# Layer 0 of a convolution-and-attention program: DVE's use of PE's products one block of taps later, spread factors copied by ACT, splits and Newton's step on DVE

## The chip, the cores and the metric

The kernel runs on one core of one Trainium2 chip. The metric is the device time of one execution in microseconds (us). One program computes both layers; nothing but inputs and the output passes the host. The engines are named as in the profile: PE (TensorE's matmuls; PEld is its weight loads), DVE (VectorE), ACT (ScalarE), POOL (GpSimd), SP (SyncE, which issues most DMAs).

## The reference

The input is eight images of 256 channels and 32 x 32 pixels, in fp32. The program computes layer 0 and then layer 1 (a causal attention over 1024 tokens and a dense feed-forward block of eight experts). The change concerns layer 0 alone:

```python
def _ln(x, w, b):                      # norm over channels, no mean subtracted
    r = lax.rsqrt(jnp.mean(x * x, axis=1, keepdims=True) + LN_EPS)
    return x * r * w[:, None, None] + b[:, None, None]

def _attention(x, ...):
    qkv = _bn(_conv1x1(x, qkv_w), ...).reshape(B, NH, 2 * KD + HD, N)   # NH 4, KD 32, HD 64, N 1024
    q, k, v = ...
    attn = softmax(einsum('bhkn,bhkm->bhnm', q, k) * SCALE)
    out = einsum('bhdm,bhnm->bhdn', v, attn).reshape(B, Cc, H, W)
    out = out + _bn(_dwconv3(v_img, pe_w), ...)        # depthwise 3x3 of v
    return _bn(_conv1x1(out, proj_w), ...)

def _edffn(x, pi_w, dw_w, fft_p, po_w):
    x = _dwconv3(_conv1x1(x, pi_w), dw_w)              # 256 -> 1024 channels, depthwise 3x3
    x = gelu(x[:, :512]) * x[:, 512:]
    x = _conv1x1(x, po_w)                              # 512 -> 256
    # every 8x8 patch: rfft2, times fft_p, irfft2
    ...

x = x + gamma1 * _attention(_ln(x, norm1_w, norm1_b), ...)
x = x + gamma2 * _edffn(_ln(x, norm2_w, norm2_b), ...)
```

## The kernel before

**Order.** Every engine call of layer 0 goes through a wrapper (`InOrder`: pe, dve, act, pool) that keeps the instructions of each engine in the order in which Python issues them; the wrapper's line, L71, is therefore the line of all of them in the profile, and groups are told apart by the names of their tiles. The order is made by generators. Each `yield` ends a step. `main_of(i)` is the main stream of image i, nearly all of it PE's work: norm2 of image i-1 (`norm2`), the spectrum of image i-2 (`spectrum`), attention of image i (`attend`) woven with the queries and keys of image i+1 (`queries_keys`), then `values(i+1)` woven with `finish(i)`, then the projection (`project`). The side stream is the depthwise convolutions on DVE: `v_conv(i)` of v, and `hidden(i-1, ...)` of the 1024 hidden channels. A tap is one `scalar_tensor_tensor` over 128 x 1024; eight of them make one channel group, and between them `open_group` issues the group's 1x1 convolution (ph) on PE, which ACT evacuates twice (into hpad and into x or conv). `level(main, side, share)` runs one step of the main stream, then draws taps from the side until the cost booked for DVE reaches `share` times that booked for PE.

**What DVE does for PE.** Between taps DVE also uses what PE has just produced. The operation is issued in the same main step as PE's matmuls, and so ahead of that step's taps:

- `rms_norm` (norm1 in `queries_keys`, norm2): the means of squares (ms) are brought to partitions by a transpose (`factors`: tpy), POOL computes the root by pow and one Newton step and splits it in two parts (r: a rounded one and the rest), PE transposes it back (`turned`: tr), spreads it over the partitions (`apply`: rbn), and DVE multiplies image, weight and spread factor (xn). `gaps` is the number of extra yields between `factors` and `turned`.
- attention: `products()` issues, one pair of key blocks behind the exponentials (pT), the products po and the sums. `close` of a chunk of 256 queries copies them (pu, ss) and returns three later steps: `turn` (PE transposes the sums, tps; DVE's reciprocal sr; ACT's accumulate, which also writes sr; POOL's split rs), `back` (PE transposes rs, trs; ACT copies it, rsT), `spread` (PE spreads the factors, rb; DVE multiplies pu and adds it to o). The four chunks' steps run within `attend`, the last chunk's in `finish`.
- `queries_keys`: each product pq is taken by ACT (hi) and DVE (lo, the rest that hi loses by rounding).
- `spectrum`: pz (PE), zf (ACT), pf (PE), gf (DVE: times the filter), py (PE), t (DVE: the residual).

**PSUM.** The pool `ps_m` has two slots of one bank, under one tag ("mm"); ph, pq, ms, tpy, tr, rbn, tps, trs, rb, tpv, pf, py and half of pp share them. A slot is free again when the last instruction that was issued for its tile is done. The scores, pz and the rest of pp lie in `ps_s`, po and the sums in `ps_o`.

Image 0 has no hidden channels beside it; `queries_keys(0)` and `values(0)` run before the loop, and a tail (norm2 of the last image, the last two spectra, and the first matrix products of layer 1) behind it.

Of the kernel before, what the change touches and what calls it, by code (L numbers as in the profile page):

```python
# [103 lines left out]
def conv_attn_hybrid_kernel(  # L104
# [340 lines left out]
    def together(main, side, ratio):  # L445
# [10 lines left out]
        for _ in side or ():  # L456
            pass

    def level(main, side, share):

        p0, d0 = pe.spent, dve.spent
        for _ in main:
            while side is not None and dve.spent - d0 < share * (pe.spent - p0):
                step = next(side, False)
                if step is None:
                    break
                if step is False:
                    side = None
        for _ in side or ():
            pass  # L470

# [4 lines left out]
    with ExitStack() as l0:  # L476
# [141 lines left out]
        def rms_norm(b, wname, xn, gaps=0):  # L618

            of = {}  # L620

            def squares(h):
                of[h] = []
                for k in range(KC):
                    sq = one.tile([P, HALF], F32, tag="full", name="sq", bufs=2)
                    act.activation(sq, t[b][:, k, h * HALF : (h + 1) * HALF], AF.Square)
                    of[h].append(sq)

            def means(h):
# [12 lines left out]

            def factors():
                yr = of.pop("yr")
                tp = ps_m.tile([P, 2, P], F32, tag="mm", name="tpy")
                for h in range(2):
                    pe.transpose(tp[:, h, :], yr[:, h, :], ident)
                y = small.tile([P, 2, nq], F32, tag="y", name="y")
                act.copy(y, tp[:, :, ::KD])

                r = of["r"] = small.tile([P, 2, 2, nq], F32, tag="r", name="r")
                a = small.tile([P, 2, nq], F32, tag="a", name="a")
                pool.tensor_tensor(a, y, mhalf.rearrange("p (a b) -> p a b", a=2), ALU.pow)
                pool.tensor_mul(y, y, a)
                pool.tensor_mul(y, y, a)
                pool.tensor_scalar(y, y, -0.5, 1.5, ALU.mult, ALU.add)
                pool.tensor_mul(a, a, y)
                pool.tensor_copy(r[:, :, 0, :].bitcast(F32R), a)
                pool.tensor_sub(r[:, :, 1, :].bitcast(F32R), a, r[:, :, 0, :])

            def turned():
                r = of.pop("r")
                tr = ps_m.tile([2 * nq, 2, P], F32, tag="mm", name="tr")
                for h in range(2):
                    pe.transpose(tr[:, h, :], r[:, h].rearrange("p a b -> p (a b)"), ident)
                of["rT"] = small.tile([2 * nq, 2, P], F32R, tag="rT", name="rT", bufs=1)
                act.copy(of["rT"], tr)

            def apply(h):
                rb = ps_m.tile([P, HALF], F32, tag="mm", name="rbn")  # L670
                for i in range(nq):
                    pe.matmul(
                        rb[:, i * P : (i + 1) * P], pick_n[:, i : i + 1].to_broadcast([2 * nq, P]), of["rT"][:, h, :],
                        start=True, stop=True,
                    )
                hs = slice(h * HALF, (h + 1) * HALF)
                for k in range(KC):
                    dve.scalar_tensor_tensor(xn[:, k, hs], t[b][:, k, hs], col(wname, k), rb, ALU.mult, ALU.mult)

            squares(0)  # L680
            yield 0.2
            means(0)
            squares(1)
            yield 1.0
            means(1)
            level()
            yield 1.0
            factors()
# [30 lines left out]
        def queries_keys(b):  # L719
# [3 lines left out]


            att[b] = {"xn": one.tile([P, KC, N], F32, tag="xn", name="xn")}
            yield from rms_norm(b, "n1w", att[b]["xn"], 1)
            for g in range(2):
                hi = one.tile([P, N], F32R, tag="hi", name="hi")
                lo = one.tile([P, N], F32, tag="lo", name="lo")
# [1 line left out]

                def take(hs, pq):
                    act.activation(hi[:, hs], pq, AF.Identity, bias=bias)
                    dve.scalar_tensor_tensor(lo[:, hs], pq, bias, hi[:, hs].bitcast(F32), ALU.add, ALU.subtract)

                yield from qkv_group(b, g, take)
                parts = att[b][g] = [dram.tile([P, N], F32, tag=f"part{g}{r}", name="part", bufs=2) for r in range(2)]
# [54 lines left out]
        def attend(b):  # L792
# [25 lines left out]
            def close(c, po, sm):  # L818
# [8 lines left out]
                def turn():  # L827
                    tp = ps_m.tile([P, nt, P], F32, tag="mm", name="tps")
                    for i in range(nt):
                        pe.transpose(tp[:, i, :], ss[:, i * P : (i + 1) * P], ident)  # L830
                    r = small.tile([P, nt, NH], F32, tag="sr", name="sr", bufs=2)
                    dve.reciprocal(r, tp[:, :, ::KD])
                    flat = r.rearrange("p a b -> p (a b)")
                    act.activation(flat, flat, AF.Copy, accum_out=accs[:, 1, b, c : c + 1])
                    rs = of["rs"] = small.tile([P, nt, 2, NH], F32, tag="rsp", name="rs", bufs=2)
                    pool.tensor_copy(rs[:, :, 0, :].bitcast(F32R), r)
                    pool.tensor_sub(rs[:, :, 1, :].bitcast(F32R), r, rs[:, :, 0, :])

                def back():
                    tr = ps_m.tile([2 * NH, QC], F32, tag="mm", name="trs")  # L840
# [21 lines left out]
            late = []  # L862

            def products():
                for one_ in late:
                    product(*one_[:4])
                    if one_[2] == nj - 1:
                        todo.extend(close(one_[4], *one_[:2]))
                late.clear()

            for c in range(N // QC):
                qs = slice(c * QC, (c + 1) * QC)
# [2 lines left out]
                for j0 in range(0, nj, 2):  # L875
                    new = []
                    for j in (j0, j0 + 1):
                        ks = slice(j * P, (j + 1) * P)
                        s = ps_s.tile([P, NH, QC], F32, tag="s", name="s")
                        for hd in range(NH):  # L880
                            pe.matmul(s[:, hd, :], kst[:, hd, ks], qst[:, hd, qs], start=True, stop=True)
                        pT = two.tile([P, NH, QC], F32, tag="pT", name="pT", bufs=4)
                        act.activation(pT, s, AF.Exp)
                        new.append((po, sm, j, pT, c))
                    products()
                    late.extend(new)
                    later()
                    yield 3.5
            products()
            att[b]["rest"] = todo  # L890
            yield 2.6
# [172 lines left out]
        def spectrum(b):  # L1064
# [19 lines left out]
            def second(z):  # L1084
                pf = ps_m.tile([P, 2, C], F32, tag="mm", name="pf")
                pe.matmul(pf, dft, z, start=True, stop=True)
                gf = two.tile([P, 2, C], F32, tag="ev", name="gf", bufs=3)
                dve.tensor_mul(gf, pf, filt.unsqueeze(1).to_broadcast([P, 2, C]))
                return gf

            def third(n, gf):
                py = ps_m.tile([P, KC, PS, 2, W // 2], F32, tag="mm", name="py")
                for g in range(KC):
                    for k in range(2):
                        pe.matmul(py[:, g, :, k, :], gf[:, k, g * P : (g + 1) * P], idft, start=True, stop=True)
                for g in range(KC):
                    tb = t[b][:, g, n * BAND : (n + 1) * BAND]
                    dve.scalar_tensor_tensor(
                        tb, py[:, g].rearrange("p r k c -> p (r k c)"), col("gam2", g), tb, ALU.mult, ALU.add
                    )  # L1100

            z, gf = {}, {}
            for n in range(nb + 2):
# [91 lines left out]
        head = weave(norm2(B - 1), spectrum(B - 2), 1)  # L1195
        while not ready2.get(B - 1):
            next(head)

        def rest():
# [682 lines left out]
```

## Time and profile before

| | |
|---|---|
| median of three runs | 3304.81 us (3293.08 to 3309.06) |
| the profiled execution | 3302.11 us, its span 3300.4 us |
| mean granted TensorE clock | 0.966 |
| PE busy | 3043.3 us, 92% of the span, 17462 instructions |
| PEld busy | 2066.2 us, 63% |
| DVE busy | 2346.7 us, 71%, 3710 instructions |
| ACT busy | 1395.4 us, 42%, 2168 instructions |
| POOL busy | 361.1 us, 11%, 482 instructions |
| DMA | 130.60 MB, 40 GB/s on average |

Layer 0 takes the first 43% of the span, to about 1420 us. In its steady state an image takes 164.6 us, from one projection's last residual to the next (648.49 to 813.06 us).

Times in lines of the profile are in us; in a line of the timeline stand the start, the duration (of all instructions if there are several, xN), the engine, the line, the operation, the tile written and the tiles read, the shape, and in brackets the engine's idle time ahead of it with the instruction that ended it. In a line of groups stand, behind the bar, the busy time, the mean duration in ns, and the group's idle time ahead with its main releaser. The granted clock is 1.00 at full speed.

### The profile page before, as it was taken

To read this page: it belongs to the slowest core of one execution; us is meant where nothing else is said; L and a number is where in the kernel's file an instruction comes from. 1 tells how busy PE (TensorE), PEld (TensorE's weight loads), DVE (VectorE), ACT (ScalarE), POOL (GpSimd) and SP (SyncE) were. 2 spreads that over 40 slices of the span, in tenths; PEclk is the share of its full clock that TensorE was granted. 3 is DMA by queue.
4 is the path that set the end of the run, shared out by engine and by line. 5 is a ranking of instruction groups with operands and counts; after the bars stand their busy time and mean duration, and the time that the engine had idled before them with its cause. 6 is when DMAs were issued, how large, how long until landed. Compare 5 with 4: busy or idle time off the path is not lost.

```text
span 3300.4 us, 43194 instructions
## 1 busy us (share of the span) xinstructions
PE 3043.3 (92%) x17462; PEld 2066.2 (63%) x17462; DVE 2346.7 (71%) x3710; ACT 1395.4 (42%) x2168; POOL 361.1 (11%) x482
## 2 busy tenths in 40 slices
PE   5998999999998998769999998999999999999999
PEld 3554555454555455346565665678777777778787
DVE  1377877787877786835544444688888877888887
ACT  2554454545454544323333332344444444444443
POOL 1121212020212010001122212400000000000000
PEclk8998999999999999879999999899999999999999
DMA  4202030303030300030111101100000000000000
GB/s 146 71 8 77 26 77 27 77 27 77 27 77 27 77 14 7 16 136 26 47 44 39 39 26 52 42 24 20 20 20 20 32 16 23 20 20 26 13 7 13
DMA packets 44596, 130.60 MB, mean 40 GB/s; under 512 B 3862, under 2 KB 12134, under 8 KB 40550
## 3 DMA queue, kind: packets, MB, share of 16 engines
q1 hardware_dynamic: 44390, 127.78, 12.5%
q8 instruction: 139, 2.28, 0.3%
q14 instruction: 67, 0.55, 0.1%
HBM read 77.17 MB, written 50.59 MB: 39 GB/s over the span
## 4 chain that ended last, share of the span: by engine, by line
PE 49%; DVE 5%; ACT 1%; POOL 1%; issue 1%; DMA 0%; SPq 0%; ACTq 0%; POOLq 0%; DVEq 0%
PE pm L71 12%; PE pa L71 12%; PE q L71 11%; PE s L71 4%; PE po L71 3%; PE pk L71 2%; PE pv L71 2%; DVE nm L71 1%; DVE zt L71 1%; DVE pr L71 1%; DVE st L71 1%; ACT pr L71 1%; PE tp L71 1%; PE tpz L71 1%; PE tpt L71 1%
## 5 line engine op out<-in xcount | busy, mean ns | idle before, releaser
L71 ACT ACTIVATE h<-h,bn_o,bn_s 128x512 f32<-128x512 f32 x384 | 308.6, 813 | 631.2 <-DVE h L71 631.1
L71 DVE SCALAR_TENSOR_TENSOR x<-hpad,vec,x 128x1024 f32<-128x1024 f32 x248 | 317.1, 1283 | 39.9 <-ACT x L71 32.9
L71 DVE SCALAR_TENSOR_TENSOR conv<-hpad,vec,conv 128x1024 f32<-128x1024 f32 x256 | 329.3, 1293 | 15.4 <-ACT conv L71 8.9
L71 PE MATMUL pm<-h,w 128*128 128x512 f32 (+1 forms) x768 | 318.2, 523 | 0.0
L71 ACT ACTIVATE pT<-s 128x1024 f32<-128x1024 f32 x256 | 247.4, 1024 | 71.8 <-PE s L71 71.8
L71 PE MATMUL po<-pT,vT 128*32 128x256 f32 x4096 | 273.6, 385 | 0.0
L71 PE MATMUL ph<-xn,piw 128*128 128x512 f32 x512 | 244.7, 615 | 3.1 <-DVE xn L71 1.6
L71 PE MATMUL s<-kk,z 128*128 128x512 f32 x512 | 243.0, 602 | 0.6 <-DVE pr L71 0.6
L71 DVE SCALAR_TENSOR_TENSOR o<-vpad,pe_w,o 128x1024 f32<-128x1024 f32 x128 | 163.6, 1283 | 45.6 <-ACT o L71 42.4
L71 PEld LDWEIGHTS pm<-h,w 128*128 128x128 f32 x768 | 146.4, 191 | 75.4 <-issue 61.8
L71 PE MATMUL s<-qst,kst 128*128 128x256 f32 x1024 | 176.0, 314 | 14.6 <-DMA kst<-part 13.2
L71 DVE TENSOR_TENSOR h<-h,wb 128x1024 f32<-128x1024 f32 x128 | 156.8, 1225 | 43.2 <-ACT h L71 43.2
L71 DVE TENSOR_TENSOR h<-pa,first 128x512 f32<-128x512 f32 x128 | 88.3, 690 | 132.6 <-PE pa L71 129.1
L71 PEld LDWEIGHTS po<-pT,vT 128*32 128x32 f32 x4096 | 120.8, 110 | 85.8 <-issue 4.1
L71 DVE TENSOR_TENSOR h<-h,first 128x256 f32<-128x256 f32 x384 | 164.5, 428 | 13.2
L71 PEld LDWEIGHTS s<-qst,kst 128*128 128x128 f32 x1024 | 137.5, 193 | 47.9 <-issue 43.2
L71 ACT ACTIVATE hpad<-ph,pi_o 128x512 f32<-128x512 f32 x126 | 86.8, 689 | 184.6 <-PE ph L71 184.3
L71 PEld LDWEIGHTS ph<-xn,piw 128*128 128x128 f32 x512 | 92.7, 194 | 109.6 <-issue 94.4
L71 PE MATMUL pz<-pow__116,hid 128*128 128x256 f32 x512 | 134.7, 418 | 26.7 <-DVE hid L71 26.7
L71 PE MATMUL sums<-pT,ones 128*32 128x256 f32 x2048 | 158.2, 381 | 0.0
L71 PE MATMUL pa<-tz,ws 128*128 128x256 f32 x512 | 154.6, 384 | 0.0
L71 PE MATMUL pa<-ze,w 128*128 128x256 f32 x512 | 153.3, 382 | 0.0
(264 smaller groups left out, 5792.7 us busy)
## 6 DMA issues: line engine op xcount, KB each, us to landing
qst<-part SPq DMA_DIRECT2D x32, 512.0 KB, 8.7
kst<-part SPq DMA_DIRECT2D x32, 512.0 KB, 15.2
t<-in_x_dram SPq DMA_DIRECT2D x8, 1024.0 KB, 4.8
part<-hi SPq DMA_DIRECT2D x16, 512.0 KB, 2.7
part<-lo SPq DMA_DIRECT2D x16, 512.0 KB, 3.0
td<-t SPq DMA_DIRECT2D x8, 1024.0 KB, 4.9
t<-td SPq DMA_DIRECT2D x8, 1024.0 KB, 4.8
ze<-zd SPq DMA_DIRECT2D x16, 512.0 KB, 3.9
```

The lines of the kernel that those rows point to most:

```text
L71: return self._tc.keep_in_program_order(method(*args, **kwargs))
```

## The change

It touches layer 0 only, in four ways.

1. DVE's operations on PE's products are put on a list (`deferred`) instead of being issued at once. `level` empties the list (`flush`) after the taps of each step; where there are no taps, `flushed` empties it ahead of each next step. Deferred are: the Newton step and the split of norm2's root, xn, lo, the reciprocal of the softmax's sums with its split, the multiply and add of `spread`, gf, and t<-py.
2. ACT copies the spread factors to SBUF (rbs, from rbn and from rb), and DVE reads them there: 64 more ACT copies of 128 x 512.
3. The split of the reciprocal moves from POOL to DVE, ahead of ACT's accumulate. The Newton step and the split of norm2's root move from POOL to DVE; pow stays on POOL. norm1's root stays on POOL. In all DVE has 112 instructions more and POOL 112 fewer; PE's number is unchanged.
4. `gaps` becomes 2 instead of 1 for norm1 and 0 instead of 2 for norm2. `products()` issues one product behind each exponential instead of two behind two, and pT has three buffers instead of four.

```diff
+    deferred = []
+
+    def flush():
+        while deferred:
+            deferred.pop(0)()
+
+    def flushed(steps):
+        for us in steps:
+            flush()
+            yield us
+
     def level(main, side, share):
...
                 if step is False:
                     side = None
+            flush()
         for _ in side or ():
             pass
...
                 pool.tensor_tensor(a, y, mhalf.rearrange("p (a b) -> p a b", a=2), ALU.pow)
-                pool.tensor_mul(y, y, a)
-                pool.tensor_mul(y, y, a)
-                pool.tensor_scalar(y, y, -0.5, 1.5, ALU.mult, ALU.add)
-                pool.tensor_mul(a, a, y)
-                pool.tensor_copy(r[:, :, 0, :].bitcast(F32R), a)
-                pool.tensor_sub(r[:, :, 1, :].bitcast(F32R), a, r[:, :, 0, :])
+
+                def root(eng):
+                    eng.tensor_mul(y, y, a)
+                    eng.tensor_mul(y, y, a)
+                    eng.tensor_scalar(y, y, -0.5, 1.5, ALU.mult, ALU.add)
+                    eng.tensor_mul(a, a, y)
+                    eng.tensor_copy(r[:, :, 0, :].bitcast(F32R), a)
+                    eng.tensor_sub(r[:, :, 1, :].bitcast(F32R), a, r[:, :, 0, :])
+
+                if gaps:
+                    root(pool)
+                else:
+                    deferred.append(lambda: root(dve))
...
+                rbs = two.tile([P, HALF], F32, tag="rbn", name="rbs", bufs=1)
+                act.copy(rbs, rb)
                 hs = slice(h * HALF, (h + 1) * HALF)
-                for k in range(KC):
-                    dve.scalar_tensor_tensor(xn[:, k, hs], t[b][:, k, hs], col(wname, k), rb, ALU.mult, ALU.mult)
+
+                def scale():
+                    for k in range(KC):
+                        dve.scalar_tensor_tensor(xn[:, k, hs], t[b][:, k, hs], col(wname, k), rbs, ALU.mult, ALU.mult)
+
+                deferred.append(scale)
...
-            yield from rms_norm(b, "n1w", att[b]["xn"], 1)
+            yield from rms_norm(b, "n1w", att[b]["xn"], 2)
...
-                    dve.scalar_tensor_tensor(lo[:, hs], pq, bias, hi[:, hs].bitcast(F32), ALU.add, ALU.subtract)
+
+                    def low():
+                        dve.scalar_tensor_tensor(lo[:, hs], pq, bias, hi[:, hs].bitcast(F32), ALU.add, ALU.subtract)
+
+                    deferred.append(low)
...
-                    r = small.tile([P, nt, NH], F32, tag="sr", name="sr", bufs=2)
-                    dve.reciprocal(r, tp[:, :, ::KD])
-                    flat = r.rearrange("p a b -> p (a b)")
-                    act.activation(flat, flat, AF.Copy, accum_out=accs[:, 1, b, c : c + 1])
-                    rs = of["rs"] = small.tile([P, nt, 2, NH], F32, tag="rsp", name="rs", bufs=2)
-                    pool.tensor_copy(rs[:, :, 0, :].bitcast(F32R), r)
-                    pool.tensor_sub(rs[:, :, 1, :].bitcast(F32R), r, rs[:, :, 0, :])
+
+                    def invert():
+                        r = small.tile([P, nt, NH], F32, tag="sr", name="sr", bufs=2)
+                        dve.reciprocal(r, tp[:, :, ::KD])
+                        rs = of["rs"] = small.tile([P, nt, 2, NH], F32, tag="rsp", name="rs", bufs=2)
+                        dve.tensor_copy(rs[:, :, 0, :].bitcast(F32R), r)
+                        dve.tensor_sub(rs[:, :, 1, :].bitcast(F32R), r, rs[:, :, 0, :])
+                        flat = r.rearrange("p a b -> p (a b)")
+                        act.activation(flat, flat, AF.Copy, accum_out=accs[:, 1, b, c : c + 1])
+
+                    deferred.append(invert)
...
-                    o = att[b]["o"][:, :, qs]
-                    dve.tensor_mul(pu, pu, rb)
-                    dve.tensor_add(o, o, pu)
+                    rbs = two.tile([P, NH // 2, QC], F32, tag="rbs", name="rbs", bufs=1)
+                    act.copy(rbs, rb)
+
+                    def divide():
+                        o = att[b]["o"][:, :, qs]
+                        dve.tensor_mul(pu, pu, rbs)
+                        dve.tensor_add(o, o, pu)
+
+                    deferred.append(divide)
...
             def products():
-                for one_ in late:
+                if late:
+                    one_ = late.pop(0)
                     product(*one_[:4])
                     if one_[2] == nj - 1:
                         todo.extend(close(one_[4], *one_[:2]))
-                late.clear()
...
-                        pT = two.tile([P, NH, QC], F32, tag="pT", name="pT", bufs=4)
+                        new.append((po, sm, j, s, c))
+                    for i, (po, sm, j, s, _) in enumerate(new):
+                        pT = two.tile([P, NH, QC], F32, tag="pT", name="pT", bufs=3)
                         act.activation(pT, s, AF.Exp)
-                        new.append((po, sm, j, pT, c))
-                    products()
+                        new[i] = (po, sm, j, pT, c)
+                        products()
...
-            yield from rms_norm(b, "n2w", xn2[b], 2)
+            yield from rms_norm(b, "n2w", xn2[b])
...
-                dve.tensor_mul(gf, pf, filt.unsqueeze(1).to_broadcast([P, 2, C]))
+                deferred.append(lambda: dve.tensor_mul(gf, pf, filt.unsqueeze(1).to_broadcast([P, 2, C])))
...
+                def put():
+                    for g in range(KC):
...
+                deferred.append(put)
...
+            flush()
             nc.sync.dma_start(t_d[b], t[b])
...
-        for _ in queries_keys(0):
+        for _ in flushed(queries_keys(0)):
...
-        for _ in values(0):
+        for _ in flushed(values(0)):
...
             next(head)
+            flush()
...
-        together(rest(), hidden(B - 1, (), (2,), alone=True), 1.0)
-        for _ in spectrum(B - 1):
+        together(flushed(rest()), hidden(B - 1, (), (2,), alone=True), 1.0)
+        for _ in flushed(spectrum(B - 1)):
```

More of the change, by code (lines that the diff above doesn't have):

```diff
@@ L647, in factors @@
                     pe.transpose(tp[:, h, :], yr[:, h, :], ident)
-                y = small.tile([P, 2, nq], F32, tag="y", name="y")
+                y = small.tile([P, 2, nq], F32, tag="y", name="y", bufs=2)
                 act.copy(y, tp[:, :, ::KD])
-                r = of["r"] = small.tile([P, 2, 2, nq], F32, tag="r", name="r")
-                a = small.tile([P, 2, nq], F32, tag="a", name="a")
+                r = of["r"] = small.tile([P, 2, 2, nq], F32, tag="r", name="r", bufs=2)
+                a = small.tile([P, 2, nq], F32, tag="a", name="a", bufs=2)
                 pool.tensor_tensor(a, y, mhalf.rearrange("p (a b) -> p a b", a=2), ALU.pow)
-                pool.tensor_mul(y, y, a)
-                pool.tensor_mul(y, y, a)
-                pool.tensor_scalar(y, y, -0.5, 1.5, ALU.mult, ALU.add)
-                pool.tensor_mul(a, a, y)
-                pool.tensor_copy(r[:, :, 0, :].bitcast(F32R), a)
-                pool.tensor_sub(r[:, :, 1, :].bitcast(F32R), a, r[:, :, 0, :])
+                def root(eng):
[9 more added lines that the diff above has]
+                    deferred.append(lambda: root(dve))
             def turned():
@@ L888, in attend @@
                     yield 3.5
+            products()
             products()
@@ L1095, in third @@
                         pe.matmul(py[:, g, :, k, :], gf[:, k, g * P : (g + 1) * P], idft, start=True, stop=True)
[L1096 to L1100, printed above, removed]
+                def put():
+                    for g in range(KC):
+                        tb = t[b][:, g, n * BAND : (n + 1) * BAND]
+                        dve.scalar_tensor_tensor(
+                            tb, py[:, g].rearrange("p r k c -> p (r k c)"), col("gam2", g), tb, ALU.mult, ALU.add
+                        )
+                deferred.append(put)
             z, gf = {}, {}
@@ L1197, in conv_attn_hybrid_kernel @@
             next(head)
+            flush()
         def rest():
```

## The prediction

> **What bounds the kernel now.** I read the table of windows first, for one period of layer 0 in the steady state (image 4: 660 to 825 us; columns: window, its length, then busy us and count of PE, PEld, DVE, ACT and POOL, granted clock, DMA share, GB/s).
>
> ```profile
> 660.00:825.00 165.00, 149.72 (x1244) 88.20 (x1243) 129.79 (x130) 82.57 (x126) 26.13 (x26) 0.96 0.19 52
> ```
>
> PE works 149.7 of 165 us; DVE 129.8, ACT 82.6. The period is PE's work plus PE's waits, so filling DVE's idle 35 us is worth nothing by itself. Second, the groups by line over 170 to 1300 us, where the idle time ahead of PE stands with what ended it:
>
> ```profile
> L71 PE MATMUL trs<-ident,rs 128*8 128x128 f32 x56 | 12.6, 313 | 55.5 <-POOL rs L71 55.5
> L71 PE MATMUL tr<-ident,r 128*8 128x128 f32 x26 | 5.8, 310 | 19.5 <-DVE gf L71 19.5
> ```
>
> 75 of PE's idle us sit at two transposes, of the softmax's inverse sums (trs) and of the norm's root (tr). Third, the timeline. Stall C, in finish():
>
> ```profile
> 787.59 3.70 PE L71 MATMUL pq<-xn,qkvw 128*128 128x512 f32 x8
> 791.13 0.38 PE L71 MATMUL tps<-ident,ss 128*128 128x128 f32 x2
> 795.76 0.20 DVE L71 RECIPROCAL sr<-tps 128x8 f32<-128x8 f32 x1
> 796.35 0.85 POOL L71 CAST rs<-sr 128x8 fp32r<-128x8 f32 x1 [1.59 <-ACT sr L71]
> 797.29 1.25 POOL L71 TENSOR_TENSOR rs<-sr,rs 128x8 fp32r<-128x8 f32 x1
> 798.59 0.59 PE L71 MATMUL trs<-ident,rs 128*8 128x128 f32 x2 [5.87 <-POOL rs L71]
> 798.98 5.52 PE L71 MATMUL pq<-xn,qkvw 128*128 128x512 f32 x8
> ```
>
> The sums are transposed at 791.5; the reciprocal starts 4.2 later, behind queued taps, then POOL takes 2.1. Behind the stall the same eight matmuls take 5.52 instead of 3.70: half the clock, 1.8 us more. Stall B, chunk 0 of attention:
>
> ```profile
> 718.73 1.25 POOL L71 TENSOR_TENSOR r<-a,r 128x8 fp32r<-128x8 f32 x1
> 719.93 0.18 POOL L71 CAST rs<-sr 128x8 fp32r<-128x8 f32 x1
> 720.19 1.11 POOL L71 TENSOR_TENSOR rs<-sr,rs 128x8 fp32r<-128x8 f32 x1
> 721.36 0.59 PE L71 MATMUL trs<-ident,rs 128*8 128x128 f32 x2 [3.03 <-POOL rs L71]
> 721.74 4.89 PE L71 MATMUL ph<-xn,piw 128*128 128x512 f32 x8
> ```
>
> The split rs stands behind norm1's root on POOL. Stall A, in norm2:
>
> ```profile
> 667.37 1.13 POOL L71 TENSOR_TENSOR r<-a,r 128x8 fp32r<-128x8 f32 x1
> 668.35 0.69 DVE L71 TENSOR_TENSOR gf<-pf,filt 128x512 f32<-128x512 f32 x1
> 669.18 0.38 PE L71 MATMUL tr<-ident,r 128*8 128x128 f32 x2 [3.25 <-DVE gf L71]
> ```
>
> The releaser shown is gf, but tr reads r, which POOL finished at 668.5. A, B and C recur in images 2 to 6 within 0.03 us; A also in image 7.
>
> **Removed: B.** Copy and subtraction of the split move to DVE, ahead of ACT's accumulate. Reciprocal and two tiny operations come behind the taps of their step, about 6.4 us after tps, and trs is reached 7.5 after it. 5 x 3.03 = 15.1. Three of the five B's are followed by a slow ph group (4.89 against 3.70): 3 x 1.2 = 3.6. Together 18.7.
>
> **Removed: C.** Three taps (1.3 each) run, then the reciprocal (0.20) and two operations of 128x8; PE arrives about 0.6 us later, a thin margin. 5 x (5.87 + 1.8) = 38.4. In image 1 the like stall is 7.20 and I leave 2.2 of it: 5.0; a 1.58 gap at 248.71 there, where the slot of rb was held by a late DVE multiply, goes with ACT's copy, with the clock behind it 4.9 in all (1.58 + 3.3). Waits of 1.02 and 0.85 elsewhere: 2. Sum of gains: 18.7 + 38.4 + 9.9 + 2 = **69**.
>
> **Added: PSUM held longer.** tps lies in the pool ps_m of two slots. Its reader is now issued after the step's taps, and two of these taps' steps issue ph matmuls that need slots of that pool. With one slot taken, a ph or the next product must wait until ACT has emptied the ph issued just before. The order of instructions shows such a wait three times an image in images 1 to 7 (the second ph or tpy behind tps of chunks 0 to 2, or the rbn there): 21. The price is that loop, seen where it already runs at the tail of layer 0 (PE's end is 1317.56, tpw starts 1319.17):
>
> ```profile
> 1317.76 0.69 ACT L71 ACTIVATE hpad<-ph,pi_o 128x512 f32<-128x512 f32 x1 [0.36 <-PE ph L71]
> 1318.34 0.77 ACT L71 ACTIVATE x<-ph,dw_o,vec 128x512 f32<-128x512 f32 x1
> 1319.17 0.66 PE L71 MATMUL tpw<-ident,lin 128*128 128x128 f32 x4 [0.56 <-ACT x L71]
> ```
>
> 1.6 us x 21 = 33.6; between 0 (ACT done in time because PE is late) and 2.5 each (ACT busy with an exp of 1.02 first). Whether the clock drops too is the open term. Gaps of 1.58 and 2.15 cost 6.8 and 3.4 us of half clock in this trace, gaps of 1.34, 1.02 and 0.85 none, and one of 3.08 none:
>
> ```profile
> 246.46:249.87 3.41, 1.83 (x13) 0.97 (x6) 3.38 (x6) 0.00 (x0) 0.00 (x0) 1.00 0.00 0
> 249.87:253.29 3.42, 3.42 (x10) 1.92 (x9) 3.35 (x4) 1.36 (x2) 0.00 (x0) 0.50 0.00 0
> ```
>
> PE was busy 1.83 of the first 3.41 us and ran the next at 0.50. Whether a gap tips the clock thus goes by where it falls in such a window. I let one in three do so, at the 1.8 of stall C: 7 x 1.8 = 12.6 (ends: 0, and 21 x 3.3 = 69). Sum: **46**.
>
> The Trainium skill ("TensorE: Matmul & The Clock Gate", Part 1 and "HAM oscillation") lets PE fall to 4/8 after an idle window of about 3.4 us and asks for no gaps over that. By it the 1.6-us gaps would cost only themselves, and the sum would be 12.6 lower; the 0.50 behind the 1.58 gap above speaks against it. The same page's "A second HAM failure mode: psum-queue depth-cycling" speaks against this change: there short idles from cycling through PSUM banks were enough to make the clock oscillate.
>
> **Moved: norm2's root (A).** pow stays on POOL (2.25), six operations go to DVE, into the flush behind seven taps: 656.23 + 7 x 1.31 = 665.4, gf 0.69, six operations of 128x8 at about 0.2 (nearest rows: the 128x8 reciprocal 0.20; ten times that on POOL is the far end), so tr at 667.2, 2.0 earlier. But both dropped yields bring rbn and py close behind tr, where pz x8 lay. Now rbn waits for ACT's rT (about 0.5), py for the new copy of rbn (586 ns plus signal, 0.9) and the second rbn for gf (1.3): 2.7. Net +0.7 x 6 = 4.2. A does not go, it is cut in pieces.
>
> **Added: 64 ACT copies of 128x512.** 64 x 0.586 = 37 us on an engine idle for half the period: hidden, except where PE stands right behind: tpv waits for rbs in finish, 0.4 x 7 = 2.8; image 0's norm and values, without taps to fill in, +1.4; the last norm2 and spectrum, +2.9. DVE gains nothing by reading SBUF: its multiply takes 706 ns on o from SBUF and 686 on rb from PSUM. Two more 128x8 operations per close and six per norm2, under 3 us an image, fall into DVE's idle 35; without that cover 8 x 3 = 24. Products issued one by one behind each exp, with three pT instead of four, and low, gf and put a flush later move no wait of PE that I could find: 0, or +1 for each of seven images. The third yield now ahead of norm1's tr gives its root, which stays on POOL, one step more. POOL's queue only gets shorter; of the DMAs only each image's store td<-t stands a flush later, and nobody waits for it: 0.
>
> **Sum.** -69 + 46 + 4.2 + 2.8 + 4.3 = -11.5, against the profiled execution's 3302.1 (span 3300.4): **3290.6 us**, -0.35%. That execution lies 2.7 below the median 3304.8. A measurement of this kernel can tell about 0.5%, 16.5 us, from no change. Layer 1 has no edit: 0.
>
> **Rivals.** *Faster*: the PSUM waits find ACT ready or cost no clock (-12.6: 3278), and A closes as well (6 x (3.24 + 1.6) = 29 less: 3249). For it: 1.34, 1.02 and 0.85 left the clock alone. Against: DVE's chain and gf in A. *Slower, one mechanism*: every PSUM wait tips the clock. At 1.8 each 21 x 1.8 = 37.8 instead of 12.6: 3316; at 3.3, 3347. It decides from 14 of the 21 on (11.5 / 1.8 = 6.4 beyond 7). For it: B tipped 3 of 5 and A also runs pz at 5.30 against 3.62. Against: 1.6 fits inside half a window. *Slower by late DVE*: the reciprocal misses C's margin of 0.6 and C stays: -11.5 + 38.4, so 3329. *Nothing happens* is the case itself: gains and new waits cancel.
>
> **How the numbers follow.** Forecast case 0.45 (own range 3282 to 3300), the faster ones 0.33 (3278: 0.23, 3249: 0.10), every wait tipping the clock 0.14, C staying 0.08. Range: 3252 leaves out most of 3249; 3330 leaves out 3347 and the upper half of C's case. Faster by over 0.5%: most of 0.33 and a fifth of 0.45, 0.38. Slower: half of 0.14, 0.08 and a little for unseen waits, 0.18. Within: 0.44.
>
> **What would show it.** Right: trs without idle ahead of it in images 2 to 6 and pq at 3.70 behind it; PE gaps of about 1.6 before ph, tpy or rbn released by ACT, three an image; tr still with gaps around it; DVE's 128x8 operations near 0.2. Wrong: trs still released by DVE at 3 us or more; PSUM gaps absent, or with 0.50 behind most; a period far from 163 (now 164.6).

## The result, and the profile after

The changed kernel takes 3314.61 us, median of 20 runs, against 3309.05 of 20 runs of the kernel before: ratio 1.0023, 95% interval 1.0014 to 1.0033. The forecast was 3290.6, 11.5 us less than before; the time rose by 5.6. It lies inside the stated range and inside the 0.5% that the prediction called the least a measurement can tell, but the interval of 20 runs lies wholly above 1: the kernel became a little slower, not faster.

The page of the changed kernel shows the moved work and nothing of a gain: 112 instructions more on DVE, 112 fewer on POOL, 64 more on ACT, and PE busy for the same share. A window of 165 us over about the same stretch of image 4 as the one shown of before has PE at work for 149.56 us, where before it was 149.72.

```profile
span 3306.7 us, 43215 instructions
...
PE 3047.5 (92%) x17462; PEld 2071.9 (63%) x17462; DVE 2366.0 (72%) x3822; ACT 1435.5 (43%) x2232; POOL 275.9 (8%) x370
```

```profile
656.30:821.30 165.00, 149.56 (x1236) 88.15 (x1235) 130.66 (x142) 87.28 (x134) 14.00 (x13) 0.96 0.19 52
```

The groups over 170 to 1300 us of the changed kernel (busy, mean ns, idle time ahead with its releasers):

```profile
L71 PE MATMUL ph<-xn,piw 128*128 128x512 f32 x448 | 210.6, 601 | 14.6 <-ACT conv L71 11.6 <-ACT x L71 2.9
...
L71 PE MATMUL py<-idft,gf 128*128 128x128 f32 x192 | 32.7, 323 | 7.0 <-ACT rbs L71 4.1 <-DVE gf L71 2.8
...
L71 PE MATMUL rbn<-rT,pick_n 8*128 8x128 f32 x104 | 21.6, 337 | 7.7 <-ACT conv L71 7.2 <-ACT rT L71 0.5
L71 PE MATMUL ms<-sq,ones 128*32 128x128 f32 x448 | 18.9, 288 | 17.9 <-ACT x L71 17.9
...
L71 PE MATMUL trs<-ident,rs 128*8 128x128 f32 x56 | 10.7, 272 | 5.3 <-DVE rs L71 5.3
L71 PE MATMUL tpy<-ident,yr 128*128 128x128 f32 x26 | 5.6, 297 | 11.1 <-ACT x L71 7.2 <-ACT yr L71 3.8
L71 PE MATMUL tr<-ident,r 128*8 128x128 f32 x26 | 5.4, 290 | 23.1 <-DVE r L71 21.6 <-ACT x L71 1.5
```

The same groups of the kernel before, those of trs and tr being shown in the prediction:

```profile
L71 PE MATMUL ph<-xn,piw 128*128 128x512 f32 x448 | 216.4, 619 | 3.1 <-DVE xn L71 1.6 <-DVE sr L71 0.8 <-ACT rsT L71 0.5
...
L71 PE MATMUL py<-idft,gf 128*128 128x128 f32 x192 | 26.6, 281 | 1.4 <-DVE gf L71 1.3
L71 PE MATMUL ms<-sq,ones 128*32 128x128 f32 x448 | 18.4, 278 | 1.2 <-ACT sq L71 0.8
L71 PE MATMUL rbn<-rT,pick_n 8*128 8x128 f32 x104 | 16.8, 281 | 3.7 <-DVE xn L71 3.2 <-ACT rT L71 0.5
...
L71 PE MATMUL tpy<-ident,yr 128*128 128x128 f32 x28 | 5.7, 285 | 3.8 <-ACT yr L71 3.8
```

B and C are gone: trs has 5.3 of 55.5 left (2.27 in image 1, 3.01 in image 7). The other rows say where the 50 us went. ms had 1.2 and has 17.9. ph, tpy and rbn had 3.1, 3.8 and 3.7 and have 14.6, 11.1 and 7.7; 28.9 us of these are 20 gaps of 1.45. tr kept its wait, and py has 7.0 instead of 1.4. The timeline of image 4, with A first:

```profile
661.25 0.17 DVE L71 TENSOR_TENSOR r<-a,r 128x8 fp32r<-128x8 f32 x1
...
661.56 0.38 PE L71 MATMUL tr<-ident,r 128*8 128x128 f32 x2 [3.37 <-DVE r L71]
...
663.98 0.59 ACT L71 COPY rbs<-rbn 128x512 f32<-128x512 f32 x1 [1.64 <-PE rbn L71]
664.62 2.08 PE L71 MATMUL py<-idft,gf 128*128 128x128 f32 x8 [0.68 <-ACT rbs L71]
...
667.67 6.25 PE L71 MATMUL pz<-pow__116,hid 128*128 128x256 f32 x16
...
698.81 1.15 ACT L71 ACTIVATE sq<-t 128x512 f32<-128x512 f32 x2 [7.89 <-DMA t<-in_x_dram]
...
702.24 0.79 ACT L71 ACTIVATE x<-ph,dw_o,vec 128x512 f32<-128x512 f32 x1
...
703.08 0.70 PE L71 MATMUL ms<-sq,ones 128*32 128x128 f32 x16 [4.51 <-ACT x L71]
...
715.39 0.44 PE L71 MATMUL tps<-ident,ss 128*128 128x128 f32 x2
715.66 1.88 PE L71 MATMUL ph<-xn,piw 128*128 128x512 f32 x4
...
718.17 0.77 ACT L71 ACTIVATE x<-ph,dw_o,vec 128x512 f32<-128x512 f32 x1
...
718.99 0.44 PE L71 MATMUL tpy<-ident,yr 128*128 128x128 f32 x2 [1.45 <-ACT x L71]
...
721.49 0.20 DVE L71 RECIPROCAL sr<-tps 128x8 f32<-128x8 f32 x1
```

Three things stand here. First, the root's last step ends at 661.42 and tr still waited 3.37. What follows runs at half clock (py 2.08 against 1.16 before, pz 6.25 against 5.30). The tables of windows, the changed kernel's first, show that this half clock lasts 10.24 us, where before it lasted 3.41; the two rows of the kernel before follow:

```profile
662.58:672.82 10.24, 9.56 (x29) 7.80 (x29) 9.12 (x12) 1.17 (x2) 0.00 (x0) 0.50 0.01 3
```

```profile
669.71:673.12 3.41, 3.41 (x10) 2.70 (x9) 3.34 (x4) 0.25 (x1) 0.00 (x0) 0.50 0.00 0
```

```profile
669.40 5.30 PE L71 MATMUL pz<-pow__116,hid 128*128 128x256 f32 x16
...
677.44 1.16 PE L71 MATMUL py<-idft,gf 128*128 128x128 f32 x8
```

Second, ACT stands for 7.89 us at sq until the load of the next image lands; the evacuation of a ph is queued behind it, and PE's ms needs that ph's slot. In the kernel before, ACT's wait at the same place was 0.56:

```profile
692.65 1.15 ACT L71 ACTIVATE sq<-t 128x512 f32<-128x512 f32 x2 [0.56 <-DMA t<-in_x_dram]
```

Third, tpy waits for ACT to empty the ph issued just before, because tps, transposed at 715.8, keeps its slot until the reciprocal at 721.49.

For the parts I use a sum over layer 0 that can be worked out from the trace: PE's time without a matmul, and the matmul time spent at half clock, of which at most half is lost. Layer 0 ends where the matmul votes starts.

| kernel (profiled execution) | layer 0 ends | PE without a matmul | matmuls at half clock |
|---|---|---|---|
| before | 1420.6 | 175.9 | 103.4 |
| changed | 1423.5 | 176.9 | 103.3 |
| before_split_on_dve | 1373.3 | 140.4 | 77.6 |
| split_and_deferred_reciprocal | 1411.1 | 172.9 | 77.3 |
| split_and_norm_steps | 1411.5 | 166.2 | 108.1 |
| split_copies_and_products | 1382.8 | 148.0 | 84.6 |
| tps_copied_out | 1411.3 | 159.6 | 109.9 |

Both columns of the changed kernel are those of before: the waits and the half clock have moved, not shrunk. Layer 1, in which nothing is edited, took between 1863.8 and 1875.1 us in these profiles (from its first transpose, tpt, to the end), so layer 0's end is the better measure of a part than the whole time.

### The profile page after: what moved, and what is told of

Its sections match the earlier page's. It is cut to its first block, busy times and chain, and to the rows that moved or that the text cites. A ratio compares the mean times of both kernels' runs of the same rounds, so it can differ in the third digit from the quotient of the medians.

```text
span 3306.7 us, 43215 instructions
## 1 busy us (share of the span) xinstructions
PE 3047.5 (92%) x17462; PEld 2071.9 (63%) x17462; DVE 2366.0 (72%) x3822; ACT 1435.5 (43%) x2232; POOL 275.9 (8%) x370
## 4 chain that ended last, share of the span: by engine, by line
PE 49%; DVE 4%; ACT 1%; POOL 1%; issue 1%; DMA 0%; SPq 0%; ACTq 0%; POOLq 0%; DVEq 0%
PE pm L71 12%; PE pa L71 12%; PE q L71 11%; PE s L71 5%; PE po L71 3%; PE pv L71 2%; PE pk L71 2%; DVE nm L71 1%; DVE zt L71 1%; DVE pr L71 1%; PE tpt L71 1%; ACT pr L71 1%; PE tp L71 1%; PE tpz L71 1%; PE pw L71 1%
## 5 line engine op out<-in xcount | busy, mean ns | idle before, releaser
L71 ACT ACTIVATE pT<-s 128x1024 f32<-128x1024 f32 x256 | 259.0, 1023 | 105.8 <-PE sums L71 74.4
L71 PE MATMUL ph<-xn,piw 128*128 128x512 f32 x512 | 239.3, 600 | 15.3 <-ACT conv L71 11.6
L71 DVE SCALAR_TENSOR_TENSOR o<-vpad,pe_w,o 128x1024 f32<-128x1024 f32 x128 | 163.7, 1283 | 47.2 <-ACT o L71 44.2
L71 PE MATMUL s<-qst,kst 128*128 128x256 f32 x1024 | 176.0, 316 | 14.8 <-DMA kst<-part 13.7
L71 PE MATMUL q<-t,ws 128*128 128x256 f32 x512 | 152.7, 380 | 0.8 <-DVE t L71 0.8
```

The source lines that it names most:

```text
L71: return self._tc.keep_in_program_order(method(*args, **kwargs))
```

## The experiments

### The causes in the changed kernel, one at a time

**tps_copied_out.** The sums leave PSUM at once:

```diff
+                    sc = small.tile([P, nt, NH], F32, tag="sc", name="sc", bufs=2)
+                    act.copy(sc, tp[:, :, ::KD])
                     def invert():
...
-                        dve.reciprocal(r, tp[:, :, ::KD])
+                        dve.reciprocal(r, sc)
```

> The changed kernel, with one ACT copy more in turn: the 128x8 sums go from tps (PSUM) to SBUF at once, and the deferred reciprocal reads them there. Slot theory (tps blocks one of the two slots of ps_m until the deferred reciprocal): the gaps of 1.45 us ahead of tpy, rbn and ph, three an image in images 2 to 7 and two in image 1, vanish, 20 x 1.45 = 29 us; the wait of 2.8 to 4.5 ahead of ms and the one of 3.4 ahead of tr stay; about 3286, ratio to before 0.993. Rival (PE waits there for ACT's lateness, not for the slot): the gaps stay and the time is that of the change, 3315; the copy, queued behind exponentials, may even hold the slot as long.

Measured: 3293.25, ratio 0.996 (0.9945 to 0.9975), 21 us less than the changed kernel. Its groups, over the same stretch:

```profile
L71 PE MATMUL ph<-xn,piw 128*128 128x512 f32 x448 | 209.8, 601 | 0.4
...
L71 PE MATMUL ms<-sq,ones 128*32 128x128 f32 x448 | 19.1, 291 | 18.6 <-ACT x L71 18.6
...
L71 PE MATMUL trs<-ident,rs 128*8 128x128 f32 x56 | 11.1, 280 | 14.8 <-DVE rs L71 14.6
```

All gaps of 1.45 are gone: a slot held too long is what they were. A third of the gain came back at trs (14.8 against 5.3): PE now arrives there earlier, and the reciprocal is where it was.

**put_at_once.** The residual goes out at once:

```diff
-                deferred.append(put)
+                put()
```

> The changed kernel, with the residual t<-py of the spectrum issued at once again, so that the store of the image, and the load of a new one into its place behind it, no longer stand behind a step's taps. Store theory: the load is issued about 5 us earlier, ACT's wait for it ahead of sq (7.9 us in image 4, 34.8 in all) falls to about 1, and PE's wait ahead of ms (2.8 to 4.5, 17.9 in all) goes: 3315 - 18 = 3297, with some clock a little less. Rival (ms waits for a PSUM slot like the others): 1.5 us stay ahead of ms, and the time moves by under 8 us.

Measured: 3314.49, ratio 1.0014 (1.0005 to 1.0023). The store theory falls: in image 4 the load was issued at 693.92 instead of 694.06, and ms waited 18.3 in all. No taps stood ahead of the deferred t<-py there. Of the rival only the time came out, not its 1.5 ahead of ms; the cause had to be another.

**norm2_two_gaps.** norm2 with its two extra steps again; which engine has the root is now an argument of its own:

```diff
-                if gaps:
+                if on is pool:
                     root(pool)
...
-            yield from rms_norm(b, "n2w", xn2[b])
+            yield from rms_norm(b, "n2w", xn2[b], 2, dve)
```

> The changed kernel, with the two extra steps of norm2 between tpy and tr put back; the root stays on DVE, deferred. Theory (the dropped steps took away the cover, pz x16, that stood ahead of tr and behind it): the wait of 3.37 ahead of tr goes in images 1 to 6, 6 x 3.4 = 20, the 0.68 and 0.56 ahead of py stay or double, and of the half clock behind it (6.8 to 13.7 us in three images of six) some 2 us an image go: 3315 - 20 - 12 = about 3283. Rival (the chain gf, root, tr just moves on: the taps of the added steps stand ahead of the flush as well): the wait ahead of tr stays at 3 us, about 3312.

Measured: 3325.5, ratio 1.0054 (1.0039 to 1.007), slower still. It told two things:

```profile
L71 PE MATMUL py<-idft,gf 128*128 128x128 f32 x192 | 27.8, 289 | 18.2 <-DVE gf L71 9.4 <-ACT rbs L71 7.3 <-DVE t L71 1.5
...
L71 PE MATMUL ms<-sq,ones 128*32 128x128 f32 x416 | 16.7, 278 | 0.0
...
L71 PE MATMUL trs<-ident,rs 128*8 128x128 f32 x56 | 11.7, 293 | 22.7 <-DVE rs L71 22.7
L71 PE MATMUL tr<-ident,r 128*8 128x128 f32 x26 | 6.2, 330 | 25.6 <-DVE gf L71 25.6
```

ms waits no more: its wait came from the two dropped steps. They move the rest of the spectrum against attention, so that norm1's squares stand closer behind the store and the load: in image 4 of the changed kernel the store is issued 41.6 us behind the projection's last residual, where before it was 31.5, and ACT comes to sq 44.2 behind it, where before it was 39.7. And A stays at 4.25 an image, B and C come back in part (1.04 and 2.48), and py waits 18.2: the deferred chain gf, root just moves on with the taps, as the rival said.

**all_three.** The three edits above together.

> All three together: tps copied out, t<-py at once, norm2's two steps back. If the three causes are separate their gains add: 29 + 18 + 32 = 79 less than 3315, about 3236, ratio to before 0.978. Rival (PE then meets DVE, which is busy for about 130 us of 165 and now issued late, or ACT): the sum falls short by half, about 3275.

Measured: 3305.33, ratio 0.9989 (0.998 to 0.9998). Neither number: the last edit's loss (11 us in its own run) takes back half of what the first gains.

**keys_one_step_later.** tps_copied_out, and in `main_of`:

```diff
-            yield from weave(steps, queries_keys(i + 1) if i + 1 < B else none(), 1)
+            yield from weave(steps, later_on(1, queries_keys(i + 1)) if i + 1 < B else none(), 1)
```

> tps_copied_out, with the queries and keys of the next image woven in one step of attention later (norm2 keeps no extra steps). Theory (the two dropped steps of norm2 brought norm1's squares one step closer behind the store and the load of the image, and ACT stands in its queue until the load lands): ACT's wait for the load ahead of sq (about 35 us in five images) falls under 6 and PE's wait ahead of ms (18.6 in all) goes: 3293 - 18 = 3275. Rival (the step is missing at the end, where the keys are stacked and the scores wait for the DMAs): ms goes but 10 us or more appear ahead of s or pq; 3290.

Measured: 3284.0, ratio 0.9925 (0.991 to 0.9939). ms has 0.0, but nearly all of its 18 us come back, as 1.45 ahead of ph and 1.27 ahead of po once an image (17 us more in these two groups). What is gained is mostly clock: 92.4 us of matmuls at half clock in layer 0 instead of 109.9, up to 8.8 us, and 4.3 us less of PE's idle time.

**root_at_once.** tps_copied_out, with

```diff
-                    deferred.append(lambda: root(dve))
+                    root(dve)
```

> tps_copied_out, with the Newton step and the split of norm2's root issued on DVE at once, ahead of the step's taps. Theory (the wait ahead of tr is the taps that stand ahead of the deferred root): DVE waits some 2.4 us for POOL's pow and then needs 1.2, so r is there about 4 us after tpy, and pz x16 (3.6) covers it: 3.38 ahead of tr falls under 0.6, 6 x 2.8 = 17, and of the half clock behind it about half, 8: 3293 - 25 = 3268. Rival (the wait moves to gf, py and rbn, which now come closer behind, or to the taps, which are 2.4 us later): the gaps there grow by as much; 3290.

Measured: 3294.08, ratio 0.9954 (0.9938 to 0.9971), nothing gained:

```profile
654.33 0.17 DVE L71 TENSOR_TENSOR r<-a,r 128x8 fp32r<-128x8 f32 x1
...
654.64 0.38 PE L71 MATMUL tr<-ident,r 128*8 128x128 f32 x2 [3.38 <-DVE r L71]
```

The wait ahead of tr is the 3.38 of tps_copied_out. It is not this step's taps that stand ahead of the root but the seven taps of the steps before it, which had waited for ACT's first product of the depthwise convolution. **all_mended** is tps_copied_out with both of the last edits.

> tps copied out, keys one step later and root at once together. If the three causes are separate: 3293 - 18 - 25 = 3250, ratio to before 0.982. Rival (DVE or ACT then sets PE's time): 3275.

Measured: 3283.65, ratio 0.9924 (0.9909 to 0.994), the time of keys_one_step_later alone.

### The parts of the change, added to the kernel before

The losses below are differences of medians. The split's own runs and those of the other four had 3310.38 and 3304.82 for the kernel before; by the ratios the losses are 39, 47, 8 and 7 us instead of 38, 43, 5 and 5.

**before_split_on_dve.** One edit of the change, nothing deferred:

```diff
-                    flat = r.rearrange("p a b -> p (a b)")
-                    act.activation(flat, flat, AF.Copy, accum_out=accs[:, 1, b, c : c + 1])
                     rs = of["rs"] = small.tile([P, nt, 2, NH], F32, tag="rsp", name="rs", bufs=2)
-                    pool.tensor_copy(rs[:, :, 0, :].bitcast(F32R), r)
-                    pool.tensor_sub(rs[:, :, 1, :].bitcast(F32R), r, rs[:, :, 0, :])
+                    dve.tensor_copy(rs[:, :, 0, :].bitcast(F32R), r)
+                    dve.tensor_sub(rs[:, :, 1, :].bitcast(F32R), r, rs[:, :, 0, :])
+                    flat = r.rearrange("p a b -> p (a b)")
+                    act.activation(flat, flat, AF.Copy, accum_out=accs[:, 1, b, c : c + 1])
```

> The kernel before, with one edit of the change alone: the two operations of the reciprocal's split on DVE instead of POOL, ahead of ACT's accumulate; nothing is deferred. Theory (the prediction's steps for B and C): B, 3.03 us in images 2 to 6, goes; of C, 5.87, the 2.1 on POOL and ACT's link go and 3.7 stay, because the reciprocal still stands behind taps; no gap of 1.45 appears. 5 x 3.0 + 6 x 2.1 = 28 us and a few of clock: about 3278, ratio 0.991. Rival (PE meets another wait right behind, so that the gain of the whole change was never to be had): gaps of the same size appear elsewhere, 3305.

Measured: **3262.28**, ratio 0.9863 (0.9844 to 0.9881). It has the lowest time of all kernels here. Its timeline of C, and its groups:

```profile
764.28 0.38 PE L71 MATMUL tps<-ident,ss 128*128 128x128 f32 x2
...
767.36 0.19 DVE L71 RECIPROCAL sr<-tps 128x8 f32<-128x8 f32 x1
...
767.98 0.17 DVE L71 TENSOR_TENSOR rs<-sr,rs 128x8 fp32r<-128x8 f32 x1
...
768.29 0.38 PE L71 MATMUL trs<-ident,rs 128*8 128x128 f32 x2 [2.41 <-DVE rs L71]
```

```profile
L71 PE MATMUL ms<-sq,ones 128*32 128x128 f32 x448 | 18.2, 278 | 0.4 <-ACT sq L71 0.3
...
L71 PE MATMUL trs<-ident,rs 128*8 128x128 f32 x56 | 11.3, 286 | 20.3 <-DVE rs L71 20.3
```

B is gone and C is 2.41 instead of 5.87: from the reciprocal's end to trs it is 0.74 us here, 2.63 before. The edit changes two things at once, the engine and the place ahead of ACT's accumulate; by the prediction's rows 2.2 of the 2.63 lay on POOL (796.35 to 798.54) and 0.4 ahead of it, and no run parts the two. No gap of 1.45 appears. PE's idle time falls by 35.5, and 25.8 us of matmuls less at half clock give up to 12.9 more: 48.4, against layer 0's 47.3. My number, 3278, was 16 too high, since C shrank by more than POOL's 2.1 and the clock gave more than "a few".

**split_and_deferred_reciprocal.** The above, with reciprocal, split and accumulate in `invert`, put on the deferred list:

```diff
+                    def invert():
...
+                    deferred.append(invert)
...
                 if step is False:
                     side = None
+            flush()
```

> before_split_on_dve (3262), with a second part of the change: reciprocal and split on the deferred list, issued behind the step's taps. Slot theory: the 20 gaps of 1.45 us ahead of tpy, ph and rbn (or pq) appear here too, without the rest of the change: +29; the rest of C (2.41) goes, 20 in all at trs: -16 and some clock: about 3275. Rival (the gaps need the other parts as well): none appear and it is 3246.

Measured: 3300.83, ratio 0.998 (0.9969 to 0.9991); 38 us of the gain are lost. The gaps of 1.45 appear, 11 of them, and five of 1.12 ahead of pq; but trs, which should have lost the rest of C, has more:

```profile
L71 PE MATMUL ph<-xn,piw 128*128 128x512 f32 x448 | 213.2, 606 | 13.7 <-ACT conv L71 10.1 <-ACT x L71 2.9 <-ACT rsT L71 0.5
...
L71 PE MATMUL pq<-xn,qkvw 128*128 128x512 f32 x192 | 99.8, 656 | 7.0 <-DVE sr L71 5.6 <-ACT conv L71 1.4
...
L71 PE MATMUL trs<-ident,rs 128*8 128x128 f32 x56 | 11.9, 298 | 29.7 <-DVE rs L71 29.7
```

C is 3.78, with seven taps queued ahead of the reciprocal. So the deferral does not by itself close C; in the changed kernel C is closed because there DVE's queue has run empty by then (it waited 0.71 us for tps), in an order that other parts of the change made.

**split_and_norm_steps.** before_split_on_dve, with norm1 at two extra steps, norm2 at none, and norm2's root (all but pow) on DVE, issued at once (as in the change, y, r and a have two buffers each instead of four):

```diff
-            yield from rms_norm(b, "n1w", att[b]["xn"], 1)
+            yield from rms_norm(b, "n1w", att[b]["xn"], 2)
...
-            yield from rms_norm(b, "n2w", xn2[b], 2)
+            yield from rms_norm(b, "n2w", xn2[b])
...
+                eng = pool if gaps else dve
-                pool.tensor_mul(y, y, a)
+                eng.tensor_mul(y, y, a)
...
```

> before_split_on_dve (3262), with norm1 at two extra steps, norm2 at none, and norm2's root on DVE behind POOL's pow, issued at once. Theory (the dropped steps bring norm1's squares too close behind the load, and strip tr of its cover): ACT waits 25 us or more for the load ahead of sq, PE some 18 ahead of ms; the wait of 3.2 ahead of tr stays, with 7 us of half clock behind it instead of 3.4: 3262 + 18 + 10 = 3290. Rival (that wait needs the deferral): ms stays under 2 and the time within 8 us of 3262.

Measured: 3305.72, ratio 1.0006 (0.9997 to 1.0015); 43 us lost, more than the 28 expected. ACT's wait for the load in image 4 (timeline), and PE's waits (groups):

```profile
694.68 1.15 ACT L71 ACTIVATE sq<-t 128x512 f32<-128x512 f32 x2 [8.54 <-DMA t<-in_x_dram]
```

```profile
L71 PE MATMUL ms<-sq,ones 128*32 128x128 f32 x448 | 18.6, 285 | 16.9 <-ACT x L71 16.9
...
L71 PE MATMUL tr<-ident,r 128*8 128x128 f32 x28 | 5.7, 289 | 19.7 <-DVE r L71 19.7
```

Nothing is deferred here, so the wait ahead of ms does not need the deferral; norm2_two_gaps had shown that it needs the dropped steps. tr waits as long as with the whole root on POOL. Idle time grows by 25.8, and 30.5 us more of matmuls run at half clock: up to 15.3 more, 41 in sum, against 38 in layer 0's end.

**split_copies_and_products.** before_split_on_dve, with ACT's 64 copies and the products one by one with three pT, as in the change's diff:

```diff
+                act.copy(rbs, rb)
...
-                for one_ in late:
+                if late:
+                    one_ = late.pop(0)
...
-bufs=4)
+bufs=3)
```

> before_split_on_dve (3262), with ACT's copies of rbn and rb (64) and the products issued one behind each exponential with three pT; nothing deferred. Theory: hidden, but for tpv and image 0, +5: 3267. Rival (PE frees the slot of rb earlier, or products come in time): -5; or the copies delay the exponentials and PE waits ahead of s: +15.

Measured: 3267.56, ratio 0.9886 (0.9871 to 0.99): 5 us lost in the medians, the number expected, though the two intervals overlap; layer 0 ended 9.5 later in the profile (1382.8). The way there was not the expected one: tpv's idle time rose by only 0.6, while py waits for rbs (11.6 in all instead of 1.4) and C is 3.26.

**split_and_three_gaps.** before_split_on_dve, with

```diff
-            yield from rms_norm(b, "n2w", xn2[b], 2)
+            yield from rms_norm(b, "n2w", xn2[b], 3)
```

> before_split_on_dve (3262), with three instead of two extra steps in norm2, an attempt at stall A. Theory: one more step of the spectrum ahead of tr covers POOL's root: 3.24 ahead of tr goes in six images, 19, and 3 to 6 of clock: 3240. Rival (the step shifts the load against norm1's squares, or gf, xn and py wait instead): 3262 or more.

Measured: 3267.26, ratio 0.9883 (0.9869 to 0.9898). A closes (tr 0.4), but py waits 2.66 for gf instead (18.9 in all) and 24 us more of matmuls run at half clock. The wait was DVE's backlog under another name. Here too the interval overlaps that of before_split_on_dve; layer 0 ended 10 later in the profile (1383.3).

## Why the prediction was wrong

Its sum was -69 + 46 + 7 + 4.3; layer 0 in the profile shows +2.9. By its steps:

- **Removed: B and C.** Right in what is idle: 50.2 of trs's 55.5 went, where the steps made 15.1 + 29.3 + 5.0. But this was counted as the change's gain as a whole. 35.2 of the 50.2 come from the split alone (before_split_on_dve), which leaves C at 2.41, and adding the deferral to it makes C longer.
- **Added: PSUM held longer.** Right in kind, place, number and price: 20 gaps of 1.45, 29 us, for 21 of 1.6. Its clock was too dear: one gap of the 20 (576.29, in image 3) has half clock behind it for one window of 3.41, where 12.6 us were put down. About 31, not 46.
- **Nobody waits for the store.** This step failed. The load of the next image stands behind the store, ACT's sq behind the load, ACT's evacuations behind sq, and PE's ms behind these: 17.9 us instead of 1.2. It wasn't the flush (put_at_once) but the two dropped steps (norm2_two_gaps, split_and_norm_steps). I had followed them only to rbn and py, and not to the order of the two streams behind norm2.
- **Moved: norm2's root (A).** That A would stay was right, and of its idle time little changed: 28.9 us about the six A's, 28.1 before. But its clock was put at nothing: the half clock lasted 6.83 to 13.65 us behind the six A's, 58 in sum, where before it was 3.41 each, 20.5. That is up to 19 us of PE's time, where the whole term was +4.2. The wait ahead of tr did not shrink either. In image 4 tr starts 7.20 behind tpy instead of 9.12, close to the 2.0 that were forecast; but PE comes to it 3.83 behind tpy instead of 5.87, because the dropped steps took a pf and a py from between. The prediction counted the first and not the second. It also read stall A as r alone, which POOL finished at 668.50; tr was released by gf, which ended at 669.04, so DVE's backlog was part of this wait already before the change.

With 31 for the slots, 16.7 for ms and 19 for A in place of 4.2 the sum is -69 + 31 + 16.7 + 19 + 2.8 + 4.3 = +4.8, against +2.9; put_at_once, whose gaps are those of the changed kernel, ends layer 0 3.2 later. That the sum comes so close is partly luck. It leaves out the half clock at four of the five waits of ms (13.6 us of matmuls, up to 6.8), while B, C and the gap at 248.71 gave back up to 23 of clock where the 69 has 16. Of the 2.8 for tpv 0.5 appeared (7.7 us of idle time ahead of it instead of 7.2), and of image 0's 1.4 nothing (PE's idle time up to 170 us is 40.0, before it was 40.7). The two terms that were too small are both of the dropped steps. Those steps and the deferral cost 43 and 38 us beside the split; the costs do not simply add, since the whole change (+52 beside before_split_on_dve) closes C, which each of the two leaves open.

"Nothing happens is the case itself: gains and new waits cancel" held; the rival that every slot wait tips the clock did not. The rule that the prediction weighed, the Trainium skill's "TensorE: Matmul & The Clock Gate", Part 1, came nearer than my one in three for the gaps of 1.45 (1 of 20). For longer ones that are still below its window of about 3.4 us it does not hold: of the five gaps of 2.41 in before_split_on_dve two have half clock about them, of the changed kernel's two of 2.78 and 2.81 ahead of ms one, and of its five A's of 3.37 all.

The traces let one read closer what goes with it. The stretches of half clock last whole multiples of 3.41 us. Cut into windows of 3.41 us that begin in step with these stretches, layer 0 of all fourteen kernels' traces has 4589 windows at full clock from about 170 us on. In 211 of them PE was at work for under 40% of the window, and half clock followed all 211; between 40 and 60% it followed 42 of 199; above that, 5 of 4179. So a gap counts by how much it takes out of one such window, as the prediction had read it: a single gap of 1.45 leaves PE at work for at least 57% of any, and the one that did tip the clock left 58%.

What stays open: how to close A. Whether the root is on POOL or on DVE, tr or the py behind it ends up waiting for DVE's backlog, by way of gf or of the root; emptying that backlog (fewer taps of v drawn ahead of norm2) wasn't tried. Nor does a run show what the other deferrals (xn, lo, gf, the multiply and add of `spread`) cost one by one: only those of the reciprocal, of norm2's root and of t<-py were tested alone.

## What to carry to other kernels

When a consumer is moved later in its engine's queue, the producer's buffer is held for that long: look first at who else needs the slot, and copy a small product out before deferring its use. When a step is dropped from a woven stream, follow everything woven behind it up to its DMAs, not only the steps next to it. And take one part alone first: here two small instructions a chunk, moved to another engine and ahead of an accumulate, were worth 1.4%, and the rest of the change spent it all.

## What was not expected of the hardware

An operation on 128x8 takes 0.17 us on DVE (the reciprocal 0.20). On POOL the same root steps took a mean of 0.34 to 1.04 us in before_split_on_dve, and near 1.2 where taps ran on DVE beside them (6 of the changed kernel's 6):

```profile
L71 POOL TENSOR_TENSOR a<-a,y 128x8 f32<-128x8 f32 x6 | 7.4, 1242 | 0.5
L71 POOL TENSOR_SCALAR y<-y 128x8 f32<-128x8 f32 x6 | 7.4, 1231 | 0.5
```

In the tail of layer 0, where DVE had no taps, the same two took 0.20 each (split_and_deferred_reciprocal, at 1292.3 us). The traces of all fourteen kernels agree: in layer 0, POOL's operations on 128x8 other than pow took 0.19 to 0.21 us in all 295 cases with no DVE operation beside them, and a median of 1.19 in the 536 that began while a tap was running. No run changes the taps alone, so that the tap is the cause is read from this and not tested by itself.
